# The order of three exponentials on ACT in a cross attention of a two-layer decoder (one core)

## The chip, the cores and the metric

The kernel runs on one core of one Trainium2 chip. Its time is the device time of one execution in microseconds (us); the median of three runs before the change is 3290.36 us (3289.35 to 3291.89). The five engines are named as the profile names them: PE multiplies matrices (PEld is its loading of weights, which runs beside the multiplying), ACT applies functions and copies, DVE and POOL do elementwise work, and SP issues transfers. PE writes its results to PSUM, a small memory of which this stage uses eight banks; ACT and DVE copy them out.

## The reference

Two decoder layers over 32 sequences of 100 tokens of 256 numbers. Each layer has a self attention, a cross attention and a feed-forward part with experts. The change touches only layer 1's cross attention, in which every token attends to 361 context vectors of 192 numbers with 16 heads of 64:

```python
xn = (x - mu) * jax.lax.rsqrt(var + LN_EPS) * ln_gamma + ln_beta
scale = DIM_HEAD ** (-0.5)
q = xn @ Wq
kv = context @ Wkv
k, v = jnp.split(kv, 2, axis=-1)
...
dots = jnp.einsum('bhnd,bhmd->bhnm', q, k) * scale
dots = jnp.where(mask, dots, -jnp.inf)
attn = jax.nn.softmax(dots, axis=-1)
out = jnp.einsum('bhnm,bhmd->bhnd', attn, v)
...
return out @ Wo + bo
```

Its output is added to `x`; the gating of the experts that follow (a norm, eight logits for each token, the largest two) is computed in the same stage of the kernel, a group of sequences later.

## The kernel before, in words

All numbers are 32-bit floats. The program is unrolled. The stage runs inside `in_order()` (L232), under which the instructions of PE, DVE, ACT and POOL stand on each engine in exactly the order in which the Python code issues them; only SP's transfers are placed freely. An engine whose next instruction must wait holds everything behind it.

**Turns and pairs.** A turn `u` is four heads of one sequence, so there are 128 turns. Two turns make a pair (`two_turns(n)`, `n` even: 64 pairs), and eight pairs make a group of four sequences. The work is a pipeline: while pair `n` has its weights turned and summed, turns `n+2` and `n+3` have their scores and exponentials made and turn `n+3` and `n+4` their keys.

**A pair, in order** (`two_turns`, `half_of`):

- *First half*, `half_of(n)`: on PE the first part of the values (L2292) and keys (L1872), their second parts (L2297, L1879), and the scores of turn `n+2` in two portions (L2320, two heads each). ACT and DVE copy the values (L2307, L2308) and the keys (L2274 on ACT, L2275 on DVE). DVE adds the mask to each head's scores and finds their extreme (L2327). ACT makes the exponential of a head and its sum (`exponentials`, L2336: an ACTIVATE and a read of the accumulator). Four such exponentials make up turn `n+2`: (portion 0, head 0), (0, 1), (1, 0), (1, 1).
- *Turning*: `turn_weights` for the turns `n` and `n+1`, whose exponentials were made a pair ago and divided by their sums since. For each of three stretches of the 361 context places PE transposes four heads into one PSUM bank (L2352). ACT copies stretches 0 and 2 out (L2359), DVE stretch 1 (L2357).
- *Second half*, `half_of(n+1)`: it begins with the odd jobs of `part_of`, then again values, keys and scores, now for turn `n+3`. In it `divided(n+2)` takes the reciprocal of the four sums on DVE (L2344) and multiplies all four heads with it on POOL (L2345).
- *Sums*: `sums` of both turns multiplies the turned weights with the values (L2370), and DVE copies the result (L2378). `sends` issues POOL's scattered writes of finished rows (L2256) for some pairs.

**Odd jobs.** Which ones a half has is set by `n` modulo 16 in `part_of` and `norms_of`. Those that matter below stand in second halves: in the second half of the pair at place 2 of a group DVE makes the statistics of a norm right after the reciprocal (L168 to L180); at place 4 eight transposes of `x` (L217) go into two banks, which DVE (L134) and ACT (L136) copy out, and statistics follow; at place 6 eight transposes of the normed rows do the same (L151 on DVE, L142 on ACT); at places 8 and 10 the queries of the next group are projected and ACT copies them (L1905). The first and the last group have only some of these.

**PSUM.** `share_psum(sc=2, mm=4)` (L2101) gives the scores two double banks and everything else four single banks ("mm"). Values take two of the four, keys two, each turned stretch one, an odd job one or two, each turn's sums one. A bank is reused once its copy is done, so PE can be held by a copy that stands late in ACT's or DVE's order.

Of the kernel before, what the change touches and what calls it, by code (L numbers as in the profile page):

```python
# [66 lines left out]
def kernel(ctx: ExitStack, tc: tile.TileContext, io: dict, out: bass.AP):  # L67
# [570 lines left out]
    def context(b):  # L638
        cb = cbuf[b % 2]
        nc.sync.dma_start(  # L640
            cb[:, 0:2, :], io["ctx"][b, 0:256].rearrange("(c p) d -> p c d", p=P)
        )
        nc.sync.dma_start(cb[:105, 2, :], io["ctx"][b, 256:S2])
        crs[b] = cb
# [161 lines left out]
    with tc.tile_pool(name="x0", bufs=2) as pool, tc.tile_pool(name="x0p", bufs=1) as fixed:  # L806
# [145 lines left out]
        def scores(b, c):  # L952

            kT, qT = kTs[b]
            ps = scs[b, c] = [mm_tile() for _ in range(2)]
            for e in range(2):
                p0 = 64 * e
                nc.tensor.matmul(
                    ps[e][:T, :NK], qT[p0 : p0 + 64, c, :], kT[p0 : p0 + 64, c, :],
                    start=True, stop=True,  # L960
                )
            if c == 1:
                kTs.pop(b)

        def exponentials(b, c, e):

            if c == 0 and e == 0:
                exs[b] = (
                    pool.tile([T, XH, NK], F32, tag="ex", name="ex"),
                    small.tile([T, XH], F32, tag="sm4", name="sm4"),  # L970
                )
            ex, sm = exs[b]
            if e == 0:
                shifted[0] = (
                    pool.tile([T, 2, NK], F32, tag="s", name="s"),
                    small.tile([T, 2], F32, tag="nmx", name="nmx"),
                )
            s, nmx = shifted[0]
            ps = scs[b, c] if e == 0 else scs.pop((b, c))
            nc.vector.tensor_tensor_reduce(  # L980
                s[:, e, :], ps[e][:T, :NK], mbuf[b % 2], 1.0, 3.4e38, ALU.add, ALU.min,
                nmx[:, e : e + 1],
            )
            nc.scalar.activation(
                ex[:, 2 * c + e, :], s[:, e, :], AF.Exp, bias=nmx[:, e : e + 1], scale=-1.0,
                accum_out=sm[:, 2 * c + e : 2 * c + e + 1],
            )

        def divided(b, c):
            ex, sm = exs[b]  # L990
            two = slice(2 * c, 2 * c + 2)
            rc = small.tile([T, 2], F32, tag="rc2", name="rc2")
            nc.vector.reciprocal(rc, sm[:, two])
            nc.gpsimd.tensor_tensor(ex[:, two], ex[:, two], bc(rc, 2, NK), ALU.mult)
# [1118 lines left out]
    def load_expert(e):  # L2113
        w1 = w5.tile([P, 2, HID], F32, tag="w1", name="w1")
        nc.scalar.dma_start(w1, io["f1_w1"][e].rearrange("(c p) n -> p c n", p=P))
        w2 = w5.tile([P, 8, D], F32, tag="w2", name="w2")
        nc.scalar.dma_start(w2, io["f1_w2"][e].rearrange("(c p) n -> p c n", p=P))
        return w1, w2
# [143 lines left out]
    with tc.tile_pool(name="x1", bufs=2) as pool:  # L2262
# [3 lines left out]
        def keys(u, part):  # L2266

            if part < 2:
                key_products(u, part)
                if part == 0:  # L2270
                    return
            ps = kTs[u]
            kT = kTs[u] = pool.tile([P, 2, S2], F32, tag="kT", name="kT")
            nc.scalar.copy(kT[:, 0, :], ps[0][:, :S2])  # L2274
            nc.vector.tensor_copy(kT[:, 1, :], ps[1][:, :S2])  # L2275

        def values(u, last, part):

            b, v0 = u // 4, 512 * (u % 4 // 2)
            cT, vb = cTs[b], vbs[u // 2]  # L2280
            if last:
                k0, kn = CCH[2]
                parts = [(slice(k0, k0 + kn), kn, v0 + 256 * e, 256) for e in range(2)]
            else:
                parts = [(slice(k0, k0 + kn), kn, v0, 512) for k0, kn in CCH[:2]]
            if part == 0:
                held[u] = [mm_tile() for _ in range(2)]
            ps = held[u]
            for e, (at, kn, c0, n) in enumerate(parts):
                half = slice(64 * e, 64 * e + 64)  # L2290
                if part == 0:
                    nc.tensor.matmul(  # L2292
                        ps[e][:kn, :n], cT[:, 0, at], x1_wa[:, 1024 + c0 : 1024 + c0 + n],
                        start=True, stop=False,
                    )
                else:
                    nc.tensor.matmul(  # L2297
                        ps[e][:kn, :n], cT[half, 1, at], x1_wbv[half, c0 : c0 + n],
                        start=False, stop=True,
                    )  # L2300
            if part == 0:
                return
            if last:
                nc.scalar.copy(vb[2][:kn, :n], ps[0][:kn, :n])
                nc.vector.tensor_copy(vb[3][:kn, :n], ps[1][:kn, :n])
            else:
                nc.scalar.copy(vb[0], ps[0])  # L2307
                nc.vector.tensor_copy(vb[1], ps[1])  # L2308
# [113 lines left out]
        def value_tiles():  # L2422
            return [
                pool.tile([P, n], F32, tag=f"vb{k}", name=f"vb{k}")
                for k, n in enumerate((512, 512, 256, 256))
            ]
# [5 lines left out]
        NU = 4 * B  # L2432
        vbs, exs, oTs, held, lowered = {}, {}, {}, {}, {}

        def part_of(n):

            g, at = n // 16, n % 16
            if g > 0 and at < 3:
                finish(g - 1, at)
            if g > 0 and at in (5, 6, 11):  # L2440
                gating(pool, g - 1, {5: 2, 6: 3, 11: 8}[at])
            if g + 1 < NG:
                if at == 7:
                    lns[g + 1] = turned(lns[g + 1])
                    qTs[g + 1] = query_tile(g + 1)
                if 8 <= at < 12:
                    for m in range(2):
                        queries(qTs[g + 1], lns[g + 1], 2 * (at - 8) + m)

        def norms_of(n):  # L2450
            g, at = n // 16, n % 16
            if g > 0 and at in (3, 4):
                gating(pool, g - 1, at - 3)
            if g > 0 and 7 <= at < 11:
                gating(pool, g - 1, at - 3)
            if g + 1 < NG and at in (5, 6):
                normed(g + 1, at - 5)

        def sends(n):
            q, m = (n - 4) // 16 - 1, (n - 4) % 16 - 8  # L2460
            if q >= 0 and m >= 0:
                send(q * G + m // 2, m % 2)
# [3 lines left out]
        def half_of(n):  # L2466

            if n == 4:
                loaded.extend(load_expert(0))
            if n >= 0 and n % 4 == 0 and n // 4 + 2 < B:  # L2470
                cTs[n // 4 + 2] = context(n // 4 + 2)
            if n >= 0:
                part_of(n)
            v, last = n + 2 - n % 2, n % 2 == 1
            if v < NU:
                if not last:
                    vbs[v // 2] = value_tiles()
                values(v, last, 0)
            if n + 3 < NU:
                keys(n + 3, 0)  # L2480
            if -1 <= n and n + 1 < NU:
                divided(n + 1)
            if n >= 0:
                norms_of(n)
            if v < NU:
                values(v, last, 1)
            if n + 2 < NU:
                scores(n + 2, 0)
                exponentials(n + 2, 0, 0)
            if n + 3 < NU:  # L2490
                keys(n + 3, 1)
            if n + 2 < NU:
                exponentials(n + 2, 0, 1)
                scores(n + 2, 1)

        def two_turns(n):

            half_of(n)
            for e in range(2):
                if n >= 0:  # L2500
                    eTs[n + e] = turn_weights(exs.pop(n + e)[0])
                if n + 2 < NU:
                    exponentials(n + 2, 1, e)
            half_of(n + 1)
            for e in range(2):
                if n + 3 < NU:
                    exponentials(n + 3, 1, e)
                if n >= 0:
                    u = n + e
                    if u % 16 == 0:  # L2510
                        oTs[u // 16] = pool.tile([P, 8, GT], F32, tag="oT", name="oT", bufs=1)
                    sums(u, eTs.pop(u), vbs[u // 2], oTs[u // 16])
                    sends(u)
# [79 lines left out]
    with tc.tile_pool(name="f1s", bufs=2, side="right") as pool, in_order(SP):  # L2593
# [118 lines left out]
        for n in range(len(units) + 2):  # L2712
# [16 lines left out]
            if n >= 16 and n % 2 == 0 and n < 32:  # L2729

                nc.gpsimd.tensor_copy(pace, hTs[units[n]][0:1, 0:1])
                for k in range(2):
# [3 lines left out]
                    else:  # L2736
                        e = n - 24 + k
# [12 lines left out]
            if n >= 42 and n % 6 == 0 and n // 6 < 7 + E:  # L2750
                e = n // 6 - 7
# [221 lines left out]
```

## Time and profile before

| | us |
|---|---|
| median of three runs | 3290.36 |
| the profiled execution | 3296.56 |
| its span, first to last instruction | 3294.8 |
| all before layer 1's cross attention | 0 to about 1536 |
| layer 1's cross attention | about 1536 to 2697 |
| the rest (experts of layer 1) | 2697 to 3294.8 |

The profile is of one execution. Its page shows the busy time of each engine and the costliest groups of instructions; further views answer who waited for whom, what ran in a given stretch, and in what order. In a timeline a line gives start, duration, engine, line of the code, operation, what is written and read, the shape and a count (equal neighbours are merged); square brackets give the engine's idle time before it and what ended it. PE's matmuls are pipelined and their ends are modelled, so PE looks busy even where a matmul waits for its bank; such a wait is seen at the weight loads (PEld) and at the distance between starts of matmuls.

### The profile page before, as it was taken

What the parts mean: (1) busy time and instruction counts of PE and PEld (TensorE: products, weight loads), DVE (VectorE), ACT (ScalarE), POOL (GpSimd) and SP (SyncE); (2) the same over time, 40 slices, a digit from 0 to 9 for tenths busy, and PEclk for the clock granted to TensorE, in tenths of its full rate; (3) what the DMA queues carried; (4) which work ended last, traced back from release to release, by engine and by line L of the source; (5) the groups of instructions that cost most, each with busy time, mean ns of one, the idle gap of its engine ahead of it and who ended that gap; (6) DMA issues with size and microseconds to landing.
All of it is one profiled execution on the core that took longest, in us unless ns stands there. A gap on an engine that the chain in (4) does not pass through costs nothing. (4 is left out here: it accounts for less than half of the span.)

```text
span 3294.8 us, 66334 instructions
## 1 busy us (share of the span) xinstructions
PE 3163.5 (96%) x25158; PEld 2158.5 (66%) x25158; DVE 1812.7 (55%) x5224; ACT 1641.7 (50%) x3705; POOL 1335.3 (41%) x1190
## 2 busy tenths in 40 slices
PE   8998999989998799999999999999999989999998
PEld 6775666656776543334666666666666658899998
DVE  6776666757886478876455555464645451011111
ACT  5665666666674456665545545454545432211111
POOL 3445888876775432201323333333333332012222
PEclk9999999999998989999999999999999999999999
DMA  9401212101012722100100100010000003456665
GB/s 301 159 15 53 53 51 56 48 2 59 25 34 64 223 79 53 30 2 15 36 17 20 34 15 25 15 30 23 18 25 21 25 22 103 134 182 188 179 189 152
DMA packets 165700, 228.71 MB, mean 69 GB/s; under 512 B 22846, under 2 KB 139618, under 8 KB 164998
## 3 DMA queue, kind: packets, MB, share of 16 engines
q1 hardware_dynamic: 133592, 185.22, 18.0%
q0 software_dynamic: 20304, 27.99, 4.0%
q10 hardware_dynamic: 11486, 11.23, 1.0%
q8 instruction: 204, 3.34, 0.4%
q14 instruction: 114, 0.93, 0.1%
HBM read 150.92 MB, written 73.41 MB: 68 GB/s over the span
## 5 line engine op out<-in xcount | busy, mean ns | idle before, releaser
L2345 POOL TENSOR_TENSOR ex<-ex,rc 100x1444 f32<-100x1444 f32 x128 | 332.3, 2596 | 697.8 <-DVE rc L2344 456.2
L2336 ACT ACTIVATE ex<-s,nmx 100x361 f32<-100x361 f32 x512 | 305.7, 598 | 116.4 <-DVE nmx L2327 115.4
L384 POOL TENSOR_TENSOR s<-s,nmx 100x800 f32<-100x800 f32 x128 | 199.9, 1563 | 204.5 <-DVE nmx L383 110.7
L1934 ACT ACTIVATE h<-sc,cols 128x800 f32<-128x800 f32 x256 | 222.6, 924 | 96.1 <-PE sc L1928 93.7
L2804 POOL DMA_INDIRECT out_x<-y,xg x53 | 82.8, 1562 | 425.7 <-DVE y L2803 232.4
L2327 DVE CUSTOM_DVE_ANT_0 s<-sc,mb 100x361 f32<-100x361 f32 x512 | 250.7, 528 | 7.6 <-PE sc L2320 7.6
L2786 ACT ACTIVATE hgT<-sc 128x1024 f32<-128x1024 f32 x53 | 54.3, 1025 | 326.5 <-PE sc L230 326.5
L2803 DVE TENSOR_SCALAR y<-mm,gx 128x256 f32<-128x256 f32 x53 | 25.7, 484 | 323.2 <-PE mm L230 323.2
L230 PE MATMUL sc<-xgT,w1b 128*128 128x128 f32 x1696 | 198.1, 275 | 0.4 <-DVE xgT L2771 0.4
L2320 PE MATMUL sc<-kT,qT 64*100 64x361 f32 x1024 | 197.6, 463 | 0.0
L230 PEld LDWEIGHTS sc<-xgT,w1b 128*128 128x128 f32 x1696 | 193.6, 192 | 0.7 <-DVE xgT L2771 0.6
L230 PE MATMUL mm<-wx,hgT 128*128 x848 | 191.6, 379 | 0.0
L2292 PE MATMUL mm<-x_wa,cT 128*128 128x512 f32 (+1 forms) x512 | 191.2, 496 | 0.0
L2308 DVE COPY vb<-mm 128x512 f32<-128x512 f32 x64 | 44.3, 692 | 251.7 <-PE mm L2297 251.7
L2352 PEld LDWEIGHTS mm<-ident,ex 100*128 100x128 f32 (+1 forms) x1536 | 144.9, 152 | 52.9 <-issue 30.2
L181 POOL TENSOR_TENSOR rs<-va,neghalf 100x4 f32<-100x4 f32 (+1 forms) x95 | 92.6, 977 | 206.9 <-DVE va L177 74.0
L1872 PE MATMUL mm<-cT,x_wa 128*128 128x361 f32 x512 | 176.3, 467 | 0.0
L2352 PE MATMUL mm<-ident,ex 100*128 100x100 f32 (+1 forms) x1536 | 169.2, 260 | 5.8 <-POOL ex L2345 5.2
L230 PEld LDWEIGHTS mm<-wx,hgT 128*128 128x128 f32 x848 | 157.2, 190 | 19.2
L2370 PEld LDWEIGHTS mm<-eT,vb 128*64 128x64 f32 (+1 forms) x3072 | 135.4, 137 | 33.6 <-issue 33.6
L2370 PE MATMUL mm<-eT,vb 128*64 128x100 f32 (+1 forms) x3072 | 148.0, 252 | 0.0
L2307 ACT COPY vb<-mm 128x512 f32<-128x512 f32 x64 | 37.5, 587 | 220.4 <-PE mm L2297 220.4
(429 smaller groups left out, 7325.6 us busy)
## 6 DMA issues: line engine op xcount, KB each, us to landing
w1b<-in_f_w SPq DMA_DIRECT2D x55, 1024.0 KB
rows_dram<-zero SPq DMA_DIRECT2D x32, 896.0 KB
cT<-in_ctxT SPq DMA_DIRECT2D x64, 180.5 KB
cT<-in_ctxT SPq DMA_DIRECT2D x128, 90.2 KB
xg<-rows_dram SPq DMA_DIRECT2D x65, 128.0 KB
y_dram<-y ACTq DMA_DIRECT2D x65, 128.0 KB
wx<-in_f_w SPq DMA_DIRECT2D x8, 1024.0 KB
xg<-sorted_dram SPq DMA_DIRECT2D x57, 132.5 KB
```

What stands on the lines that cost most here:

```text
L181: nc.gpsimd.tensor_tensor(rs[:np_, :n], va[:np_, :n], neghalf[:np_, :n], ALU.pow)
L230: nc.tensor.matmul(ps, lhsT[k], rhs[k], start=(k == 0), stop=(k == n - 1))
L384: nc.gpsimd.tensor_tensor(sm, sm, bc(nmx, 2, T), ALU.add)
L1872: nc.tensor.matmul(kTs[u][c][:, :S2], x1_wa[:, m * P : (m + 1) * P], cT[:, 0, :], start=True, stop=False,)
L1934: nc.scalar.activation(h1, both[r2][:, :, :GT], AF.Tanh, bias=col("a1_b1", o))
L2292: nc.tensor.matmul(ps[e][:kn, :n], cT[:, 0, at], x1_wa[:, 1024 + c0 : 1024 + c0 + n], start=True, stop=False,)
L2320: nc.tensor.matmul(ps[:T, e, :S2], qT[p0 : p0 + 64, m, tok], kT[p0 : p0 + 64, c, :], start=True, stop=True,)
L2327: nc.vector.tensor_tensor_reduce(s[:, e, :], ps[:T, e, :S2], mb, 1.0, 3.4e38, ALU.add, ALU.min, nmx[:, e : e + 1],)
L2336: nc.scalar.activation(ex[:, 2 * c + e, :], s[:, e, :], AF.Exp, bias=nmx[:, e : e + 1], scale=-1.0, accum_out=sm[:, 2 * c + e : 2 * c + e ...
L2345: nc.gpsimd.tensor_tensor(ex, ex, bc(rc, 2, S2), ALU.mult)
L2352: nc.tensor.transpose(pt[:kn, j * T : (j + 1) * T], ex[:, j, k0 : k0 + kn], ident[:T, :T])
L2370: nc.tensor.matmul(po[64 * e : 64 * e + 64, m * T : (m + 1) * T], vb[k][:kn, v0 + 64 * h : v0 + 64 * h + 64] if k < 2 else vb[2 + u % 2][: ...
```

## The change

In the first half of a pair, exponential (0, 1) of turn `n+2` is no longer issued in `half_of`; and the exponentials (0, 1), (1, 0) and (1, 1) are issued together after both calls of `turn_weights`. Second halves keep the old order (`last` is true there). ACT's order between the copy of the keys and the second half was: (0, 1), copy, copy, (1, 0), copy, copy, (1, 1). It becomes: copy, copy, copy, copy, (0, 1), (1, 0), (1, 1). The number of instructions and their sizes are the same, the orders on PE, DVE and POOL are the same, and no transfer is among the moved instructions.

```diff
             if n + 2 < NU:
-                exponentials(n + 2, 0, 1)
+                if last:
+                    exponentials(n + 2, 0, 1)
                 scores(n + 2, 1)
 
         def two_turns(n):
 
             half_of(n)
-            for e in range(2):
-                if n >= 0:
+            if n >= 0:
+                for e in range(2):
                     eTs[n + e] = turn_weights(exs.pop(n + e)[0])
-                if n + 2 < NU:
-                    exponentials(n + 2, 1, e)
+            if n + 2 < NU:
+                for c, e in ((0, 1), (1, 0), (1, 1)):
+                    exponentials(n + 2, c, e)
             half_of(n + 1)
```

## The prediction

> **What bounds the kernel now.** I first read the busy times by stretch, for the whole stage and for one pair without odd jobs (PE, PEld, DVE, ACT, POOL, then PE's clock, DMA share, GB/s).
>
> ```profile
> 1536.00:2697.00 1161.00, 1155.15 (x8380) 733.76 (x8378) 631.90 (x2108) 583.78 (x1674) 402.48 (x214) 1.00 0.08 22
> 1947.90:1963.23 15.33, 15.33 (x122) 9.68 (x120) 7.77 (x27) 8.08 (x25) 7.27 (x4) 1.00 0.14 39
> ```
>
> PE bounds the stage at full clock; ACT has work for half of it. The starts of PE's single matmuls confirm it: nearly every clean pair takes 15.33 us, and its matmuls stand at the same places within 10 ns. So an exponential costs nothing in itself. What counts is where PE waits for a bank, which the waits of the weight loads show (total, times, longest).
>
> ```profile
> PEld mm L2352 <- ACT eT L2359: 11.4, 62, 0.2
> PEld mm L2292 <- DVE eT L2357: 5.6, 27, 0.2
> PEld mm L1872 <- ACT lnT L142: 1.6, 7, 0.2
> PEld mm L2292 <- ACT kT L2274: 0.2, 1, 0.2
> ```
>
> The first is what the change can remove: once a pair, PE's transposes wait for ACT's copy of a turned stretch. The others mark places where PE is only just not held. Then the timeline of the clean pair.
>
> ```profile
> 1948.05 0.44 ACT L2274 COPY kT<-mm 128x361 f32<-128x361 f32 x1
> 1948.39 0.60 ACT L2336 ACTIVATE ex<-s,nmx 100x361 f32<-100x361 f32 x1
> ...
> 1948.98 0.87 ACT L2359 COPY eT<-mm 128x400 f32<-128x400 f32 x2
> ...
> 1949.08 0.57 DVE L2357 COPY eT<-mm 128x400 f32<-128x400 f32 x1
> 1949.51 0.84 PEld L2352 LDWEIGHTS mm<-ident,ex 100*128 100x128 f32 x8 [0.18 <-ACT eT L2359]
> 1949.74 0.61 ACT L2336 ACTIVATE ex<-s,nmx 100x361 f32<-100x361 f32 x1
> ...
> 1950.33 0.89 ACT L2359 COPY eT<-mm 128x400 f32<-128x400 f32 x2
> ...
> 1951.09 0.62 ACT L2336 ACTIVATE ex<-s,nmx 100x361 f32<-100x361 f32 x1
> 1951.59 0.22 ACT L2336 ACTIVATION_READ_ACCUMULATOR ex<-s,nmx 100x1 f32 x1
> 1951.90 0.18 DVE L2344 RECIPROCAL rc<-sm 100x4 f32<-100x4 f32 x1 [1.21 <-ACT ex L2336]
> ```
>
> The first copy stands behind the exponential of 1948.39, ends at 1949.46, and 0.05 later PE's held load runs. The last exponential's sum is read by 1951.81, and the reciprocal waits for it. Last, three places where a late ACT or DVE meets PE: pair place 6, pair place 2, and the late pair at 2648.
>
> ```profile
> 1893.54 0.70 ACT L142 ACTIVATE lnT<-mm,cols 128x400 f32<-128x400 f32 x1
> ...
> 1894.29 0.38 PEld L1872 LDWEIGHTS mm<-cT,x_wa 128*128 128x128 f32 x2 [0.23 <-ACT lnT L142]
> ```
>
> ```profile
> 1863.86 0.41 DVE L2305 COPY vb<-mm 105x256 f32<-105x256 f32 x1
> ...
> 1865.41 0.44 ACT L2274 COPY kT<-mm 128x361 f32<-128x361 f32 x1
> ...
> 1866.25 0.30 PEld L2292 LDWEIGHTS mm<-x_wa,cT 128*128 128x128 f32 x2
> ```
>
> ```profile
> 2657.23 0.44 ACT L2274 COPY kT<-mm 128x361 f32<-128x361 f32 x1
> ...
> 2657.72 0.30 PEld L2292 LDWEIGHTS mm<-x_wa,cT 128*128 128x128 f32 x2 [0.23 <-ACT kT L2274]
> ```
>
> At 1894.29 PE's load follows 0.05 after ACT's copy of the normed rows (end 1894.24); at 2657.72 it follows 0.05 after ACT's copy of the keys (end 2657.67). These are dependences, and PE has no slack at either. At 1866.25 it is the same load, with ACT's copy ended 0.40 before.
>
> **Part 1, copies earlier: the gain.** Nothing is added or removed; three ACTIVATEs with their reads (about 0.6 and 0.2 us each) pass four copies on ACT's queue. They issue no transfer, and POOL's and SP's orders stay. Without the exponential ahead, the first copy starts when its transposes are done (last matmul ends 1948.46 in the trace's single records, 0.04 more for the signal) and the keys' copy has ended (1948.49), about 1948.55; it ends at 1949.03, and the held load (1949.28 would be its own pace) no longer waits. The next bank, for the sixth stretch, is the one that ACT's second copy frees: its load starts at 1949.91, 0.05 after that copy's end. The second copy's input is ready at 1949.22; with its 0.50 it now ends at 1949.72, so this load starts at 1949.77: 0.14 earlier. A smaller stall, 0.04 at the values behind, goes too in most pairs. I take 0.165 a pair, between 0.14 and 0.18.
>
> **Part 2, exponentials later: the tail.** ACT's fourth copy needs the last transposes, which now end at 1950.38; with 0.04 for the signal it runs 1950.41 to 1950.92. The first of the three exponentials starts 0.13 before a copy's end (as at 1951.09), hence at 1950.80; the next follow at the 0.585 of consecutive exponentials (1956.07 and 1956.65 in the second half). The third starts at 1951.97, and its sum is read by about 1952.66, against 1951.81: **ACT and the reciprocal are 0.85 us later**. Behind the reciprocal on DVE stands the copy of the values, in clean pairs at 1953.33, so a reciprocal at 1952.75 to 1952.93 is hidden; without that gap it would cost up to the 0.85. POOL's multiplication moves to 1953.08 to 1955.67, and its output is wanted at 1963.23. Where statistics make POOL late as well, the second turn's multiplication ends about 1.0 before PE wants it (1872.22 against 1873.28 in the next pair), still more than 0.85.
>
> **Part 3, where the tail meets PE.** All these are net against before, by absolute times in the pair.
>
> - Place 6 (seven pairs): ACT's copy of the normed rows starts 0.10 after the last read begins, at +4.65 from the first transpose instead of +3.78, ends +5.35. Two values banks and two of these fill all four, so the second key product must have this one. It starts at +5.40 instead of +4.72, and its second matmul is 0.09 slower when PE restarts (397 against 303 ns between starts): **0.77**.
> - Place 4 (seven pairs): the same with the 0.51 copy of L136, end +5.16, product +5.21 instead of +4.72, and 0.09: **0.59**.
> - Place 2 from the second group on, and place 4 of the first (eight pairs): DVE's statistics run without a gap from the reciprocal to the values' copy at 1863.86, and mask, exponential and keys' copy follow closely. All are 0.85 later: the keys' copy ends at 1866.70 instead of 1865.85, PE's load starts at 1866.75 instead of 1866.25: **0.50**.
> - The pair at 2648, the same chain without slack: **0.85**.
>
> The other 40 of 63 pairs have no such job, or queries, whose two copies have 0.3 us and more to spare.
>
> **Sum.** 40 x 0.165 = 6.6 gained; 8 x 0.50 + 7 x 0.59 + 7 x 0.77 + 0.85 = 14.4 lost; **+7.8 us**. The profiled execution took 3296.56 us (span 3294.8 and 1.8 around it), 6.2 above the median, and would take 3304.3; the sum is a difference within one stage, so I add it to the median: **3298.1 us**.
>
> By the Trainium skill (Perfetto Trace Analysis, Identifying the Most-Contended Engine) headroom of the tensor engine is judged by the share of LDWEIGHTS, not by matmul busy time. The clean pair has 9.68 of 15.33 us, which by that rule leaves over 5 us for a late copy to vanish in, and the sum would be 63 x -0.165 = -10.4 us. The row speaks against it: loads stand 0.05 behind late copies and matmuls keep their places within 10 ns; I go by the row.
>
> **The rivals.**
>
> - *The sixth stretch takes DVE's bank.* Which free bank a tile gets is settled at compile time. If it becomes the one that DVE's copy of 1949.08 frees (end 1949.65), the load starts at 1949.70 and the tail is 0.06 shorter. Gain 40 x 0.235 = 9.4; losses 8 x 0.44 + 7 x 0.53 + 7 x 0.71 + 0.79 = 13.0: +3.6, **3294.0 us**, within the measurement. For it: that copy is done first already. Against: the trace before shows the other bank.
> - *The tail stays off PE (faster).* If the loads at places 2, 4 and 6 did not need the late copies, 63 x 0.165 remains: **3280.0 us**. It would need a tail under about 0.2 us at place 4 and under 0.4 at place 2, or other banks; the 0.05 steps above speak against it.
> - *No gain.* If the fifth or sixth stretch still waits, for instance because ACT's earlier copies are held by something else, only the losses stay: +14.4, **3304.8 us**. Against: the copies' inputs are ready by the records.
>
> That the order isn't what the code says is out: ACT's timeline before follows it instruction by instruction.
>
> **How the numbers follow.** Forecast 0.50, own range 3296 to 3301 from 0.14 to 0.18 of gain and 0.1 us on the losses; DVE's bank 0.25; no gain 0.17; tail hidden 0.08. A change of 0.2% (6.6 us) is about what a measurement of this kernel tells from none: slower means over 3296.9. Slower: 0.39 of the forecast, 0.16 of no gain, 0.02 of the DVE bank: 0.57. Same: 0.34, the rest of these. Faster: 0.09. The range runs from 3291 (DVE's bank with losses 3 us smaller) to 3304 (nearly no gain), leaving out the hidden tail and the edges.
>
> **What would show it.** In the changed profile: the wait of L2352 for ACT's copies (11.4 us) mostly gone, clean pairs at 15.16 us; reciprocals 0.85 us later; new waits of L1872 for L142 and L136 of 0.5 to 0.8 us, seven times each; L2292 waiting 0.5 us for L2274 at place 2. I am wrong if pairs at places 2, 4 and 6 don't lengthen, or if clean pairs don't shorten.

## The result and the profile after

The changed kernel takes 3300.5 us against 3291.9 us of the kernel before (medians of eight executions each). The ratio is 1.0023 with a 95% interval of 1.0013 to 1.0033, so by the ratio it is slower by 7.6 us on 3291.9. The profiled execution took 3301.90 us.

Whole times are a coarse ruler here: the start of the stage alone lies between 1542 and 1550 us in the executions below, although the code ahead of it is the same. Inside layer 1's cross attention a pair whose order is the same keeps its length within about 0.01 us from one execution to the next, so I measure there. The exceptions are the pairs 58, 82 and 122 and the end of the stage, as told below; they move a stage by up to 1.3 us and about 0.5 us. A pair's length is the time from its first transpose (L2352) to that of the next pair; the stage runs from the first transposes of pair 0 to those of the last turn. Before it takes 1147.04 us, after 1154.08: **+7.04 us**. By place in the group:

| pairs | number | after minus before, us each | sum | predicted each |
|---|---|---|---|---|
| without such odd jobs, and places 8 and 10 | 39 | -0.167 | -6.52 | -0.165 |
| place 2 from the second group on, place 4 of the first | 8 | +0.264 | +2.11 | +0.50 |
| place 4 from the second group on | 7 | +0.561 | +3.93 | +0.59 |
| place 6 | 7 | +0.757 | +5.30 | +0.77 |
| the late pair (n = 120) | 1 | +0.84 | +0.84 | +0.85 |
| the end: pair 124 and pair 126 up to its second turn | 2 | +0.31, +1.08 | +1.39 | -0.165, none |

The waits of PE's weight loads after the change (total, times, longest):

```profile
PEld mm L2352 <- POOL ex L2345: 9.8, 7, 6.5
PEld mm L1872 <- ACT lnT L142: 9.2, 7, 1.3
PEld mm L1872 <- ACT gT L136: 7.8, 7, 1.1
...
PEld mm L2370 <- DVE vb L2305: 2.8, 9, 0.7
PEld mm L2292 <- DVE kT L2275: 2.3, 8, 0.3
```

The wait of L2352 for ACT's copy of a turned stretch (11.4 us, 62 times) is gone. The wait of L1872 for L142 grew from 1.6 to 9.2 us; those for L136, for the values' copy L2305 and for DVE's copy of the keys L2275 have replaced smaller ones or are new. The total of a wait counts the load's idle time, some of which passes beside matmuls; what a pair pays stands in the table.

A clean pair, as busy times in a stretch (PE, PEld, DVE, ACT, POOL, then PE's clock, DMA share, GB/s), and the start of the same pair in the timeline:

```profile
1946.86:1962.01 15.15, 15.15 (x122) 9.74 (x120) 7.77 (x27) 8.40 (x25) 7.11 (x4) 1.00 0.14 40
```

```profile
1946.88 2.31 PEld L2352 LDWEIGHTS mm<-ident,ex 100*128 100x128 f32 x24 [0.53 <-issue]
...
1947.04 0.44 ACT L2274 COPY kT<-mm 128x361 f32<-128x361 f32 x1
...
1947.54 0.49 ACT L2359 COPY eT<-mm 128x400 f32<-128x400 f32 x1
...
1948.20 0.89 ACT L2359 COPY eT<-mm 105x400 f32<-105x400 f32 x2 [0.17 <-PE mm L2352]
...
1949.39 0.49 ACT L2359 COPY eT<-mm 105x400 f32<-105x400 f32 x1 [0.31 <-PE mm L2352]
1949.78 0.60 ACT L2336 ACTIVATE ex<-s,nmx 100x361 f32<-100x361 f32 x1
...
1950.37 0.59 ACT L2336 ACTIVATE ex<-s,nmx 100x361 f32<-100x361 f32 x1
...
1950.95 0.59 ACT L2336 ACTIVATE ex<-s,nmx 100x361 f32<-100x361 f32 x1
...
1951.44 0.19 ACT L2336 ACTIVATION_READ_ACCUMULATOR ex<-s,nmx 100x1 f32 x1
...
1951.73 0.18 DVE L2344 RECIPROCAL rc<-sm 100x4 f32<-100x4 f32 x1 [2.27 <-ACT ex L2336]
```

The view now shows all 24 transposes as one block. In the single records one load in it, the first of the sixth stretch, still starts 0.05 us after the end of ACT's second copy (1948.69), but 0.14 earlier in the pair than before. The first copy starts 0.66 us after the first transpose, and the three exponentials stand behind the fourth copy. Counted from the first transpose, at 1946.88, the reciprocal comes at +4.85; before it came at +4.00. The losses in the table come from that 0.85 us, but for 0.55 us at the end. Place 6, where ACT's copy of the normed rows is the next instruction on ACT's queue:

```profile
1892.91 0.68 ACT L142 ACTIVATE lnT<-mm,cols 128x400 f32<-128x400 f32 x1
...
1893.64 0.30 PEld L1872 LDWEIGHTS mm<-cT,x_wa 128*128 128x128 f32 x2 [1.31 <-ACT lnT L142]
1893.64 0.87 PE L1872 MATMUL mm<-cT,x_wa 128*128 128x361 f32 x2 [0.74 <-ACT lnT L142]
```

The load follows the copy's end (1893.59) by 0.05, as it did before, and PE now stands idle for 0.74. Place 2, where the lateness goes through DVE:

```profile
1859.46 0.18 DVE L2344 RECIPROCAL rc<-sm 100x4 f32<-100x4 f32 x1 [2.27 <-ACT ex L2336]
...
1862.38 0.41 DVE L2305 COPY vb<-mm 105x256 f32<-105x256 f32 x1
...
1862.85 1.06 PEld L2370 LDWEIGHTS mm<-eT,vb 128*64 128x64 f32 x24 [0.26 <-DVE vb L2305]
...
1863.62 0.52 DVE L2275 COPY kT<-mm 128x361 f32<-128x361 f32 x1
...
1863.93 0.44 ACT L2274 COPY kT<-mm 128x361 f32<-128x361 f32 x1
...
1864.20 0.30 PEld L2292 LDWEIGHTS mm<-x_wa,cT 128*128 128x128 f32 x2 [0.29 <-DVE kT L2275]
```

The load of 1864.20 starts 0.06 after DVE's copy of the keys and 0.17 before ACT's has ended (1864.37), so here it doesn't need ACT's bank. The pair pays in two steps: the sums of its second turn (L2370) wait for the values' copy, which leaves them 0.28 us later than in a clean pair, and the wait for the keys' copy adds 0.16. In the late pair the load does need ACT's bank:

```profile
2660.10 0.44 ACT L2274 COPY kT<-mm 128x361 f32<-128x361 f32 x1
...
2660.59 0.30 PEld L2292 LDWEIGHTS mm<-x_wa,cT 128*128 128x128 f32 x2 [0.52 <-ACT kT L2274]
```

The end of the stage, which I had not priced. First the timeline of before, then that of after:

```profile
2684.80 2.60 POOL L2345 TENSOR_TENSOR ex<-ex,rc 100x1444 f32<-100x1444 f32 x1 [7.03 <-DVE rc L2344]
...
2690.82 0.99 POOL L2256 DMA_INDIRECT sorted_dram<-x,pos  x1 [2.22 <-DMA sorted_dram<-x,pos]
2691.83 2.60 POOL L2345 TENSOR_TENSOR ex<-ex,rc 100x1444 f32<-100x1444 f32 x1
```

```profile
2688.34 2.60 POOL L2345 TENSOR_TENSOR ex<-ex,rc 100x1444 f32<-100x1444 f32 x1 [7.87 <-DVE rc L2344]
...
2690.99 1.11 PEld L2352 LDWEIGHTS mm<-ident,ex 100*128 100x128 f32 x12 [0.62 <-POOL ex L2345]
...
2694.91 0.99 POOL L2256 DMA_INDIRECT sorted_dram<-x,pos  x1 [2.77 <-DMA sorted_dram<-x,pos]
2695.92 2.60 POOL L2345 TENSOR_TENSOR ex<-ex,rc 100x1444 f32<-100x1444 f32 x1
...
2698.58 2.06 PEld L2352 LDWEIGHTS mm<-ident,ex 100*128 100x128 f32 x12 [6.48 <-POOL ex L2345]
```

The last pairs have no scores of later turns to fill PE, so the multiplication of the last two turns on POOL sets the pace. Its first one stands behind the late reciprocal. Its second one stands behind two scattered writes, the second of which waits until the first has landed. Between the two multiplications lie 7.03 us before and 7.58 after. So 0.85 (the tail) and 0.55 (a longer landing) make 1.40, against 1.39 measured.

### The profile page after: what moved, and what is told of

Read it like the earlier page. It is cut to its first block, busy times and chain, and to the rows that moved or that the text cites. A ratio compares the mean times of both kernels' runs of the same rounds, so it can differ in the third digit from the quotient of the medians.

```text
span 3300.2 us, 66334 instructions
## 1 busy us (share of the span) xinstructions
PE 3158.1 (96%) x25158; PEld 2158.3 (65%) x25158; DVE 1811.9 (55%) x5224; ACT 1660.1 (50%) x3705; POOL 1335.5 (40%) x1190
## 5 line engine op out<-in xcount | busy, mean ns | idle before, releaser
L1872 PE MATMUL mm<-cT,x_wa 128*128 128x361 f32 x512 | 180.0, 470 | 8.9 <-ACT lnT L142 5.2
L2352 PEld LDWEIGHTS mm<-ident,ex 100*128 100x128 f32 (+1 forms) x1536 | 143.0, 152 | 47.1 <-issue 30.7
L2352 PE MATMUL mm<-ident,ex 100*128 100x100 f32 (+1 forms) x1536 | 160.0, 258 | 7.3 <-POOL ex L2345 6.7
L2370 PEld LDWEIGHTS mm<-eT,vb 128*64 128x64 f32 (+1 forms) x3072 | 136.4, 138 | 36.4 <-issue 33.0
L2370 PE MATMUL mm<-eT,vb 128*64 128x100 f32 (+1 forms) x3072 | 150.7, 253 | 1.0 <-DVE vb L2305 0.5
L1872 PEld LDWEIGHTS mm<-cT,x_wa 128*128 128x128 f32 x512 | 96.1, 190 | 78.2 <-issue 26.3
```

Of the source, the lines that this page charges most:

```text
L1872: nc.tensor.matmul(kTs[u][c][:, :S2], x1_wa[:, m * P : (m + 1) * P], cT[:, 0, :], start=True, stop=False,)
L2352: nc.tensor.transpose(pt[:kn, j * T : (j + 1) * T], ex[:, j, k0 : k0 + kn], ident[:T, :T])
L2370: nc.tensor.matmul(po[64 * e : 64 * e + 64, m * T : (m + 1) * T], vb[k][:kn, v0 + 64 * h : v0 + 64 * h + 64] if k < 2 else vb[2 + u % 2][: ...
```

## Experiments

Theory: the whole gain comes from taking exponential (0, 1) out from ahead of ACT's first copy; the whole loss is the 0.85 us by which ACT and the reciprocal are late, paid one to one where PE waits for what stands behind them, and nowhere else. Rivals: the gain or the loss belongs to the other two exponentials; PE has slack, and the pairs at places 2, 4 and 6 lengthen for another reason than the tail. All stage differences are of one profiled execution each, against the one execution of before in the table above.

**Only the later two exponentials moved.** Exponential (0, 1) keeps its place ahead of the copies.

```diff
             if n + 2 < NU:
-                if last:
-                    exponentials(n + 2, 0, 1)
+                exponentials(n + 2, 0, 1)
                 scores(n + 2, 1)
...
-                for c, e in ((0, 1), (1, 0), (1, 1)):
+                for c, e in ((1, 0), (1, 1)):
                     exponentials(n + 2, c, e)
```

> One part of the change alone: exponential (0, 1) stays ahead of the copies as before, only (1, 0) moves behind the second turn's copies. Theory (the gain comes from taking (0, 1) from in front of the first copy): the clean pairs keep 15.29 to 15.33 us (at most the 0.04 stall at the values goes), the wait of L2352 for ACT's copies stays at about 11 us, the tail is 0.42 us, place 6 loses 0.32, place 4 0.13, place 2 at most 0.06; the stage is 2 to 4 us longer than before. Rival (the gain comes from the second turn's copies being earlier): clean pairs at about 15.16.

Stage +3.53 us. Clean pairs are 0.03 to 0.04 shorter, places 8 and 10 unchanged, place 2 +0.06, place 4 +0.12, place 6 +0.32, the late pair +0.41. The waits of PE's loads:

```profile
PEld mm L2352 <- ACT eT L2359: 11.4, 62, 0.2
PEld mm L1872 <- ACT lnT L142: 5.1, 7, 0.7
...
PEld mm L1872 <- ACT gT L136: 3.8, 7, 0.5
PEld mm L2292 <- ACT kT L2274: 2.2, 9, 0.5
```

The first line is that of before, to the digit, so that wait hangs on (0, 1) alone. The other two exponentials give tail, and of a clean pair's gain of 0.18 us only 0.035. The last line is of the eight pairs at place 2 and the late pair: here the load at place 2 starts 0.05 after ACT's copy of the keys, and in the changed kernel 0.05 after DVE's. The order on PE is the same, so which of the two banks this product gets differs from kernel to kernel.

**A longer tail.** Exponential (1, 1) is made twice, the second time writing the same values over the first.

```diff
-                for c, e in ((0, 1), (1, 0), (1, 1)):
+                for c, e in ((0, 1), (1, 0), (1, 1), (1, 1)):
                     exponentials(n + 2, c, e)
```

> The changed kernel with the exponential (1, 1) made twice (the second writes the same values again), so that the tail is 0.585 us longer and nothing ahead of it moves. Theory (the losses are the tail, one to one, where PE has no slack): 23 pairs (places 2, 4, 6 and the late one) 0.585 longer each, 13.5 us, and about 1.2 at the end of the stage, clean pairs unchanged: the stage 14 to 15 us longer than in the changed kernel, 21 to 22 over before. Rival (the losses come from another dealing of the banks, not from the length of the tail): the stage within 3 us of the changed kernel. Rival (the tail costs everywhere): 63 x 0.585 = 37 us longer.

Stage +24.34 us, 17.3 above the changed kernel. The tail grew more than I had reckoned. ACT's timeline of a clean pair:

```profile
1955.36 0.60 ACT L2336 ACTIVATE ex<-s,nmx 100x361 f32<-100x361 f32 x1
...
1955.95 0.58 ACT L2336 ACTIVATE ex<-s,nmx 100x361 f32<-100x361 f32 x1
...
1956.53 0.58 ACT L2336 ACTIVATE ex<-s,nmx 100x361 f32<-100x361 f32 x1
1957.01 0.19 ACT L2336 ACTIVATION_READ_ACCUMULATOR ex<-s,nmx 100x1 f32 x1
1957.24 0.60 ACT L2336 ACTIVATE ex<-s,nmx 100x361 f32<-100x361 f32 x1
```

The third follows the second by 0.58, the repeated one follows by 0.71, and starts 0.04 after the read of the same sum has ended. The reciprocal comes at +5.57, which is 0.72 later than in the changed kernel. Against that kernel the pairs at place 2 (but pair 82, at +0.45), place 4, place 6 and the late pair are all 0.72 longer; clean pairs are unchanged to 0.01, and the seven pairs at place 8 and the first at place 10 lose 0.13 because ACT's copy of the queries (L1905) is now late too (8 waits, 2.2 us). So PE has no slack at these places, and much elsewhere; my expected size was wrong only by the pitch of the repeated exponential. This is the run that speaks most plainly against reading room out of the weight loads' share, as told below.

**The new order only where nothing stands behind.** Places 2, 4 and 6 and the late pairs keep the old order.

```diff
+        def met(n):
+            g, at = n // 16, n % 16
+            return (at == 2 and g > 0) or (at == 4) or (at == 6 and g + 1 < NG) or n in (120, 124)
...
-                if last:
+                if last or met(n):
                     exponentials(n + 2, 0, 1)
...
-            if n >= 0:
-                for e in range(2):
+            for e in range(2):
+                if n >= 0:
                     eTs[n + e] = turn_weights(exs.pop(n + e)[0])
-            if n + 2 < NU:
+                if n + 2 < NU and met(n):
+                    exponentials(n + 2, 1, e)
+            if n + 2 < NU and not met(n):
                 for c, e in ((0, 1), (1, 0), (1, 1)):
```

> The new order only in the pairs whose tail is free; the old order at place 2 from the second group on, at place 4, at place 6 where rows are turned, and in the pairs 120 and 124. Theory (gain and loss add up pair by pair): the clean pairs keep their 0.17 to 0.18, the pairs with the old order go back to their times of before: 6.5 us faster than before, ratio 0.9980. Rival (a pair's order changes its neighbours): some of the restored pairs stay longer or clean ones lose their gain, and the sum is not -6.5.

Stage -6.37 us; time 3286.5 against 3295.2, ratio 0.9969 (0.9958 to 0.9980). The pairs put back are within 0.008 of before, the clean ones keep their whole gain. Of the wait that the change removes, the pairs put back keep their share:

```profile
PEld mm L2352 <- ACT eT L2359: 4.4, 24, 0.2
```

Gain and loss are thus independent of one another, pair by pair, and the change's idea is sound in 39 pairs of 63.

**The norm's statistics ahead of the reciprocal.** In second halves DVE makes the statistics before it waits for ACT's sums.

```diff
+            if n >= 0 and last:
+                norms_of(n)
             if -1 <= n and n + 1 < NU:
                 divided(n + 1)
-            if n >= 0:
+            if n >= 0 and not last:
                 norms_of(n)
```

> The changed kernel with the odd jobs of norms_of in second halves issued ahead of the reciprocal and its multiplication, so that DVE makes the statistics while the tail runs. Theory (at place 2 the tail reaches PE through the reciprocal and the statistics behind it): place 2, the first group's place 4 and the pair at place 8 of the last group go to 0.15 to 0.18 shorter than before (were 0.26 and 0.84 longer), place 4 and 6 of the other groups stay 0.56 and 0.76 longer; the stage 2 to 4 us longer than before. Rival (place 2 is held by ACT's later exponentials themselves, or by POOL): place 2 stays at +0.26.

Stage +0.59 us. Place 2 goes from +0.26 to -0.18 (pair 82 to -0.47), the late pair from +0.84 to -0.29; places 4 and 6 stay (+0.56, +0.75), as they must if they hang on ACT's queue and not on DVE's. So place 2 now gains as much as a clean pair. The late pair gains 0.11 more than that, the idle time that it had lost already in before: there its load waited for ACT's copy of the keys, which here ends 1.9 us earlier. Some 1.3 us of the stage lie in three pairs (58, 82, 122): in them the transposes of before, and of the changed kernel too, wait for ACT's copy of the keys (L2274, three times, 1.1 us in all), and here they don't. In 58 and 82 the wait is missing under "A longer tail" and "The odd copies on DVE" too, in 122 only where the statistics come first; the cause stays open. Without the three the stage is at +1.9, just below what I expected. The statistics themselves took less time as well, which the timelines show, first of before and then of this run:

```profile
1861.26 2.60 POOL L2345 TENSOR_TENSOR ex<-ex,rc 100x1444 f32<-100x1444 f32 x1 [6.33 <-DVE rc L2344]
...
1863.26 0.62 DVE L177 TENSOR_SCALAR va<-mv 100x4 f32<-100x4 f32 x1
1863.79 0.16 DVE L180 TENSOR_SCALAR sh<-mv 100x4 f32<-100x4 f32 x1
```

```profile
1856.43 0.17 DVE L177 TENSOR_SCALAR va<-mv 100x4 f32<-100x4 f32 x1
1856.51 0.16 DVE L180 TENSOR_SCALAR sh<-mv 100x4 f32<-100x4 f32 x1
```

Four numbers a row take 0.62 us, and 0.17 where POOL is idle. Before, that instruction ended at 1863.88, and POOL's multiplication at 1863.86. No run shows what this saving alone is worth to PE, because place 2 comes out no better than a clean pair.

**Exponential (0, 1) between the two turns' copies.** The other two stay behind.

```diff
-            if n >= 0:
-                for e in range(2):
+            for e in range(2):
+                if n >= 0:
                     eTs[n + e] = turn_weights(exs.pop(n + e)[0])
-            if n + 2 < NU:
-                for c, e in ((0, 1), (1, 0), (1, 1)):
-                    exponentials(n + 2, c, e)
+                if n + 2 < NU:
+                    if e == 0:
+                        exponentials(n + 2, 0, 1)
+                    else:
+                        exponentials(n + 2, 1, 0)
+                        exponentials(n + 2, 1, 1)
```

> Exponential (0, 1) moved only behind the first turn's two copies, (1, 0) and (1, 1) behind the second turn's: the first two copies are as early as in the changed kernel, but one exponential less is left behind the last copy. Theory (the gain is the first two copies', the loss is the length of the tail): clean pairs 0.17 to 0.18 shorter as in the changed kernel, tail 0.33 instead of 0.85 us, so place 2 is 0.17 shorter than before too, place 4 longer by 0.0 to 0.1 and place 6 by 0.2 to 0.3, the late pair by 0.3: the stage 5 to 6 us shorter than before, ratio 0.998. Rival (all four copies have to be ahead for the gain): clean pairs gain less than 0.1, the stage within 2 us of before.

Stage -3.15 us, where I had expected 5 to 6 us of gain; 3290.55 against 3295.04, ratio 0.9987 (0.9976 to 0.9997). The gain of the pairs without losses is kept in full (on average -0.18, at places 8 and 10 -0.15). The tail is 0.43 (reciprocal at +4.43), where I had reckoned 0.33, and what follows is larger by as much: place 4 +0.145, place 6 +0.34, the late pair +0.42. Place 2 is at -0.155: a tail of 0.43 costs it nearly nothing, one of 0.85 costs 0.44 against a clean pair, so its slack is about 0.4. At the end pair 126 pays +0.92, of which 0.39 is a longer landing of the scattered write (7.42 us between the multiplications).

```profile
PEld mm L1872 <- ACT lnT L142: 6.0, 7, 0.9
PEld mm L1872 <- ACT gT L136: 4.7, 7, 0.7
```

**The odd copies on DVE.** In the changed kernel, `transposed` gives both copies of places 4 and 6 to DVE, so that ACT's late queue holds no bank there.

```diff
-    def transposed(dst, src, gain=None, bias=None, tiles=None):
+    def transposed(dst, src, gain=None, bias=None, tiles=None, dve=False):
...
+            if dve and gain is None:
+                turn[0] += 1
+                nc.vector.tensor_copy(dst[:, c, :], ps[c][:, :GT])
+            elif dve:
+                turn[0] += 1
+                nc.vector.tensor_scalar(
+                    dst[:, c, :], ps[c][:, :GT], col(gain, c), col(bias, c), ALU.mult, ALU.add
+                )
...
+        transposed(lnT, ln, "x1_g", "x1_b", tiles=mm_tile, dve=len(x1_pools) > 1)
...
+            transposed(gT, xs[g], tiles=mm_tile, dve=True)
```

> The changed kernel with both copies of the odd job at places 4 and 6 on DVE, ahead of the reciprocal that waits for the tail anyway, instead of the second one on ACT behind the exponentials. Theory (these places lose because that copy stands behind the tail): places 4 and 6 go from 0.56 and 0.76 longer to 0.1 to 0.2 shorter than before, place 2 stays 0.26 longer: the stage 4 to 5 us shorter than before, ratio 0.9986. Rival (they lose by the tail in another way, through the reciprocal or the statistics): place 6 stays more than 0.3 longer.

Stage -6.29 us; 3292.24 against 3295.04, ratio 0.9991 (0.9980 to 1.0003). Places 4 and 6 go from +0.56 and +0.76 to -0.25 each; place 2 stays at +0.26 (but pair 82), the late pair at +0.84 and the end at +1.35. So the loss at places 4 and 6 is ACT's late copy alone. These pairs are 0.25 ahead of before in the changed kernel too, up to the load that waits for the copy, since their odd transposes (L217) come earlier as well; the late copy itself thus costs 0.81 and 1.01 us. Some 0.5 us of the stage's gain lie in the pairs 58 and 82.

**All three together.** Exponential (0, 1) between the copies, statistics first, odd copies on DVE (lines are 8 further down here).

> A version to beat both: (0, 1) between the two turns' copies, both odd copies on DVE, norms ahead of the reciprocal. Theory: nothing waits for the short tail any more, all 62 full pairs are 0.14 to 0.18 shorter, 0.3 us or so are lost at the end of the stage: 10 to 11 us shorter than before, ratio 0.9968. Rival (norms ahead of the reciprocal make POOL's multiplication late): some pairs at places 2 to 4 or 8 wait for it, and the stage gains less than 7 us.

Stage -12.00 us; 3282.65 against 3295.04, ratio 0.9969 (0.9957 to 0.9980). Every pair up to 124 is shorter, those without such odd jobs and at places 8 and 10 by 0.12 to 0.19 (58 and 122 by more), places 4 and 6 by 0.21, the late one by 0.29; only the last, 126, loses (+0.63). Some 1.3 us lie again in pairs 58, 82 and 122. The two largest waits of PE's loads that are left in the stage and have an instruction that ended them:

```profile
PEld mm L2360 <- POOL ex L2353: 6.8, 3, 6.0
PEld mm L2300 <- DVE oT L2386: 6.5, 27, 0.2
```

No wait for ACT's odd copies of places 4 and 6 is left. This version is faster than before, the interval lying below 1; its whole time is no better than that of the mixed order above (the intervals are the same), but its stage is 5.6 us shorter.

## Why the prediction was right

Its forecast, 3298.1 us or +7.8, stands against +7.6 by the ratio and +7.04 by the stage. That the number is closer than its steps is luck, for two of them failed in opposite directions.

- *What bounds the kernel, and part 1.* Right. PE sets the pace, and the one wait a pair was worth 0.167 us (0.165). The sixth stretch's load came 0.14 earlier, as worked out: 0.05 after the end of ACT's second copy, and 0.11 after that of DVE's, so the rival of DVE's bank is out. Moving two exponentials with (0, 1) in place left the wait whole, which shows which of the three carried it.
- *Part 2.* Right to the digit: 0.85 us, from the fourth copy's end and the 0.585 between exponentials.
- *Part 3, places 4 and 6 and the late pair.* Right in mechanism and size: 0.56, 0.76 and 0.84 against 0.59, 0.77 and 0.85. The longer tail raised them one to one, the shorter tail lowered them by as much, and giving the copies to DVE removed the first two. The rival in which the tail stays off PE is out. The 0.09 for the second product after PE's restart rests on no row of before, though: there two of these products always start 303 or 304 ns apart, and 397 is the step from the last of them to L2297. After the change the step at the 14 places is 407 or 408, so this term came out by luck.
- *Part 3, place 2.* Mechanism right, size wrong: 0.264 instead of 0.50, 1.9 us over eight pairs. The failed step is "the keys' copy ends at 1866.70 instead of 1865.85, PE's load starts at 1866.75": I took the bank of the late pair, which ACT's copy frees, for that of place 2. There the load of the changed kernel waits for DVE's copy of the keys, which ends 0.23 before ACT's. In the trace of before both copies had ended when the load ran, so it didn't show which was needed, and with only the later two exponentials moved it was ACT's after all; the step should have had both ends. The step also left out the earlier wait on this path, that of the sums for the values' copy.
- *The sum.* It counted pair 124 as clean and stopped ahead of the last turn. The end costs 1.39 instead of gaining 0.165: there PE waits for POOL's multiplication, and the forecast's own sentence that the multiplication is hidden (wanted at 1963.23, done at 1955.67) holds only while a later turn fills PE. 0.85 of it is the tail. The other 0.55 is a longer landing of a scattered write. In the seven experiments the distance between the two multiplications was from 0.04 us shorter to 0.52 longer than before, and from 0.14 to 0.52 longer in the three that are built on the changed order there (one with an exponential more), so whether the order of the exponentials has a part in that stays open.
- *Headroom.* The Trainium skill (Perfetto Trace Analysis, Identifying the Most-Contended Engine) judges the tensor engine's headroom by MFU, the share of its peak that it computes at, and the busy share of the weight loads. Room for a late copy can't be read out of the latter: before, a pair at place 2 and a clean one both have loads for 9.68 of 15.33 us, and yet the longer tail cost the first 0.72 us and the second at most 0.01. The -10.4 us that such a reading gives is out; the measurement decides.

## What to carry to other kernels

When instructions are moved back in an in-order queue, list what stands behind their new place in every variant of the loop body, and look for the load that starts a constant 0.05 us after such an instruction: where there is one, the lateness is paid whole, and elsewhere it is free up to the slack there (about 0.4 us at place 2), so the same edit can gain in 39 pairs and lose in the other 24. Price it by pair and by place, because a whole time of 3300 us doesn't resolve a few us, and price the first and last turns of a pipeline apart, for the cover is missing there. A loss of that kind can often be taken away at its place (here by giving a copy to the other engine, or by putting DVE's waiting instruction last) while the gain is kept.

## What the runs showed of the hardware

- A small DVE instruction can last until POOL's large one has ended: L177, four numbers a row, took 0.62 us beside POOL's multiplication, ended 0.02 after it, and took 0.17 when moved to where POOL was idle. The Trainium skill (SBUF — State Buffer, Who interferes with whom) has it that some DVE operations and POOL lock a shared pair of ports against each other for a whole instruction; these rows agree with it, though no run here tells the port from another shared resource. In the late pair an addition of 100x8 numbers (L2208) lasted 2.45 us beside that multiplication, before and after the change, and 0.17 with POOL idle (the statistics first).
- Two exponentials that write different places follow each other in 0.585 us. The repeated one, which writes the same places, followed in 0.71, its start 0.04 after the end of the first one's read.
- The two copies of the keys, on DVE and on ACT, end 0.23 us apart at place 2. That the next load of the changed kernel follows the earlier of them accounts for the 0.24 by which the loss there fell short of the forecast. With only the later two exponentials moved, it follows the later one.
